# Layer 1's softmax sums taken from the product itself, its result turned by VectorE, and another order of tokens

## The chip, the cores and the metric

The kernel runs on one NeuronCore of a Trainium2 chip. The metric is the device time of one execution in microseconds (us), the median of several runs. Everything is float32. TensorE (PE) multiplies, VectorE (DVE) and ScalarE (ACT) do the elementwise work, GpSimd (POOL) does a few small operations, and SyncE (SP) issues every DMA of the program, one after the other in program order.

## The reference, cut to what is computed

Two layers over 4 images of 128 channels and 4096 places. Layer 0 is attention over the places with a gate and a projection; layer 1 is attention of the normalised tokens with themselves, and then a recurrent step over time.

```python
# layer 0
vg = sigmoid(conv_bn(gn(x), Wvg));  v, gate = split(vg)
q = conv_bn(gn(x), Wq) * SCALE;     k = conv_bn(gn(x), Wk)
attn = softmax(q^T k);              out = (v attn^T) * gate
x = x + conv_bn(out, Wp, sp, bp)
# layer 1
t = to_tokens(x)                                   # (4, 4096, 128)
h = layernorm(t);  q = h @ W;  t = t + softmax(q q^T) @ h
t = t + ffn(layernorm(t))                          # Wx, batch norm, y = sigmoid(wx_t + y V^T)
x = from_tokens(t)
```

Two facts are used below. Layer 1's scores are symmetric, so the exponentials of block (n, a) turned over are those of block (a, n). And a row of `h` is a layer norm without gain or bias, so its 128 channels sum to zero.

## The kernel before, in words

Each image b goes through `layer0` and then `layer1`; a recurrence over all images (from L814 on) ends the program. The 4096 places are 8 blocks of 512 (`QB`), each 4 tiles of 128.

`layer0` (L402 to L496) is a loop over query blocks n and 16 pairs of key tiles. Each pair is two score products into `ps` (L231), one exponential over 128x1024 (L233, ACT), a running sum of it (L240, DVE) and four products with the values into `o` (L426). After a block, `finish` (L433) appends six closures to the list `pending`, and later rounds of the loop take one each: `sums`, `denominators`, `projection`, `tokens`, and two called `nothing`, which give their place to the list `ahead` (preparation of the next image). `tokens` makes the tokens `t`, stores them to DRAM (L484) and writes their layer norm to `h`. Three times in a block, `move` (L263) turns a 128x512 tile over: DVE transposes 32x32 blocks into `d` (L269), one DMA writes `d` to a DRAM tile (L274), and four DMAs read it back in another order (L276). SP waits for the write before it issues the reads.

`layer1` (L498 to L740) goes over query blocks n in the order 6, 7, 5, 4, 3, 2, 1, 0 and over the key blocks a from n down to 0, with two rounds for each pair (n, a). A round has two score products (L695), two exponentials of 512 columns which also leave their row sums in `slots` (L701), and two products into `o` (L562) which lag two rounds behind. For a < n the exponentials are also turned over: DVE transposes them into `dd` (L706), 16 DMAs on SP carry `dd` to `tt` (L735), and four rounds later `reversed_products` makes four products with `tt` (L575), and DVE adds up all of `tt` for the other half of the softmax sums (L580). On the diagonal (a = n) the second round is `quarter` (L524), which computes a part of the scores and copies the rest from the round before.

`count` (L595) counts the parts of block n's output and its sums; when all are in, `finish` (L602) appends to `pending`: `tokens` (four transposes of the output L631, sum of `slots` L627, reciprocal, division and residual L633, layer norm), `result` (four transposes of the tokens by PE L644, an ACT copy L647, one DMA to `t2_d` L648), two `nothing`, `turn` (four transposes of the layer norm L653, an ACT copy L654) and `inputs` (one product L658, statistics L659, a copy L665 and its DMA L666). In the last image the blocks n < 4 have no `nothing`.

The program's text is not the order of an engine's instructions: a scheduler places them from priorities when the kernel is built, and each engine then runs its list in order.

Of the kernel before, what the change touches and what calls it, by code (L numbers as in the profile page):

```python
# [18 lines left out]
P = 128  # L19
# [30 lines left out]
def conv_attn_hybrid_kernel(  # L50
# [17 lines left out]
    turn_d = [dram.tile([P, 4, NQ, 32], F32, name=f"turn{i}_d") for i in range(8)]  # L68
# [60 lines left out]
    def scales():  # L129

        nc.vector.tensor_mul(w_v, w_v, bc[:, 0, :])
        nc.vector.tensor_mul(w_p, w_p, bc[:, 2, :])

        nc.vector.tensor_scalar(par2, par[:, SG : BG + 1], 0.5, None, ALU.mult)
# [31 lines left out]
def fast(  # L166
# [13 lines left out]
    with ExitStack() as st:  # L180
# [82 lines left out]
        def move(blocks, dst):  # L263

            nonlocal n_moves
            d = work.tile([P, 4, NQ, 32], F32, tag="d", name="d", bufs=2)
            turned = nc.vector.transpose(d.rearrange("q a j i -> q j a i"), blocks)  # L269
            if n_moves == 0:  # L270
                tc.keep_in_program_order(turned)
            via = turn_d[n_moves % len(turn_d)]
            n_moves += 1
            nc.sync.dma_start(via, d)  # L274
            for a in range(4):
                nc.sync.dma_start(dst[bass.ts(a, 32)], via[:, a].rearrange("(p i) j k -> i p j k", p=4))  # L276
# [18 lines left out]
        def tiles(t):  # L295

            return [t[:, :, j, :] for j in range(NQ)]

# [112 lines left out]
        def layer0(b, gate, q, k, v, need):  # L411
# [20 lines left out]
            def finish(n, o, acc):  # L432
# [12 lines left out]
                sub = stat.tile([P, NQ, 4], F32, tag="sub", name="sub", bufs=2)  # L445

                def sums():


                    half, blocks = acc[:, 0, :], acc[:, 1, :]  # L450
                    nc.vector.tensor_tensor(half, half, blocks, ALU.add)
                    nc.vector.transpose(blocks, half)
                    nc.vector.tensor_reduce(
                        sub, blocks.rearrange("q (j f k) -> q j f k", j=NQ, f=4), AX.X, ALU.add
                    )
                    move(xb.rearrange("c (j f k) -> c j f k", j=NQ, f=4), t)

                def denominators():
                    m0, m1 = halves(quart, sub.rearrange("q j f -> q (j f)"))
                    tot = stat.tile([P, NQ, 4], F32, tag="tot", name="tot", bufs=2)  # L460
                    flat = tot.rearrange("q j f -> q (j f)")
                    nc.vector.tensor_copy(flat, m0)
                    nc.vector.tensor_tensor(flat, flat, m1, ALU.add)
                    nc.vector.tensor_tensor(
                        tot, tot,
                        own.rearrange("q (j f) -> q j f", j=1).to_broadcast([P, NQ, 4]), ALU.mult,
                    )
                    den = den_all[:, b * NT + n * NQ : b * NT + (n + 1) * NQ]
                    nc.vector.tensor_reduce(den, tot, AX.X, ALU.add)
                    nc.vector.reciprocal(rinv, den)  # L470

                def projection():
# [3 lines left out]
                    move(og.rearrange("c (j f k) -> c j f k", j=NQ, f=4), yt)  # L476

                def tokens():
                    for j in range(NQ):
# [7 lines left out]
                    move(  # L487
                        h[:, ts, :].rearrange("q j (p i) -> q j p i", p=4),
                        qt[:, cs].rearrange("c (p j k) -> c p j k", j=NQ, p=4),
                    )  # L490
# [7 lines left out]
        def layer1(b, h, qt):  # L498
# [7 lines left out]

            slots = accp.tile([P, NT, NB + 1], F32, tag="slots", name="slots", bufs=2)
            nc.gpsimd.memset(slots[:, :, NB:], 0.0)
# [14 lines left out]
            def quarter(n, ps, e, before, slots):  # L523
# [14 lines left out]
                for half in range(2):  # L538
                    at = NQ * n + 2 + half
                    nc.scalar.activation(  # L540
                        e[:, half, hb:], ps[:, 0, bass.ts(half, hb)], AF.Exp, bias=shift,
                        accum_out=slots[:, at, n : n + 1],
                    )
                for half in range(2):
                    at = NQ * n + 2 + half
                    nc.scalar.activation(
                        e[:, half, :hb], ps[:, 1, bass.ts(half, hb)], AF.Identity,
                        accum_out=slots[:, at, NB : NB + 1],
                    )

            def order(n):


                return [1, 0] if b == B - 1 and n == 0 else list(range(n, -1, -1))
# [15 lines left out]
            def reversed_products():  # L570
# [3 lines left out]
                for j in range(NQ):  # L574
# [5 lines left out]
                nc.vector.tensor_reduce(  # L580
                    slots[:, bass.ts(n, NQ), a], t.rearrange("q p b k j -> q b p (k j)"),
                    AX.XY, ALU.add,
                )
                part(a, ot)
                count(n)

            def part(n, o):
# [5 lines left out]
                count(n)  # L593

            def count(n):  # L595


                parts[n] += 1
                if parts[n] == NB - (b == B - 1 and n == 0):
                    finish(n)  # L600

            def finish(n):  # L602
# [3 lines left out]
                if b == B - 1 and n == 0:  # L606
# [3 lines left out]
                    th, t2 = two[:, 0, :], two[:, 1, :]  # L610
# [3 lines left out]
                else:  # L614
# [3 lines left out]
                    t2 = None  # L618
# [5 lines left out]
                def tokens():  # L624
                    at = (B + b) * NT + n * NQ
                    den = den_all[:, at : at + NQ]
                    nc.vector.tensor_reduce(den, slots[:, bass.ts(n, NQ), :], AX.X, ALU.add)  # L627
                    nc.vector.reciprocal(rinv, den)
                    m = bank().rearrange("q (j c) -> q j c", j=NQ)
                    for j in range(NQ):  # L630
                        nc.tensor.transpose(m[:, j, :], oacc[:, n, bass.ts(j, P)], ident)  # L631
                    for j in range(NQ):
# [7 lines left out]
                def result():  # L640
                    nonlocal t2
                    m = bank()
                    for j in range(NQ):
                        nc.tensor.transpose(m[:, bass.ts(j, P)], t1[:, j, :], ident)  # L644
                    if t2 is None:
                        t2 = work.tile([P, QB], F32, tag="xb", name="t2")
                    nc.scalar.copy(t2, m)  # L647
                    nc.sync.dma_start(t2_d[b, :, cs], t2)  # L648

                def turn():  # L650
# [3 lines left out]
                    nc.scalar.copy(th, m)  # L654
# [13 lines left out]
                if b == B - 1 and n == 0:  # L668
                    pending.appendleft(tokens)
                    pending.extend([result, turn, inputs])  # L670
                elif b == B - 1 and n < 4:
                    pending.extend([tokens, result, turn, inputs])
                else:
                    pending.extend([tokens, result, nothing, nothing, turn, inputs])


            for n in [NB - 2, NB - 1] + list(range(NB - 3, -1, -1)):
# [4 lines left out]
                for a in order(n):  # L682
# [4 lines left out]
                    for i in range(2):  # L687
                        ps = ps_s.tile([P, 2, QB], F32, tag="s", name="ps")
                        e = ep.tile([P, 2, QB], F32, tag="e", name="e")
                        if a == n and i == 1:  # L690
                            quarter(n, ps, e, before, slots)
                        else:
                            for half in range(2):
# [4 lines left out]
                                )  # L698
                            for half in range(2):
                                at = NQ * a + 2 * i + half  # L700
                                nc.scalar.activation(  # L701
                                    e[:, half, :], ps[:, half, :], AF.Exp, bias=shift,
                                    accum_out=slots[:, at, n : n + 1],
                                )
# [19 lines left out]
                        if a > n and i == 1:  # L724
                            count(a)
# [571 lines left out]
```

## Time and profile before

| what | value |
|---|---|
| time, median of 3 runs | 3062.62 us (3060.75 to 3062.82) |
| the run that was profiled | 3064.04 us, span in the profile 3062.2 us |
| granted TensorE clock | 0.992 of full speed |
| ACT, busy | 1151.9 us (38%) |
| POOL, busy | 149.0 us (5%) |
| DMA moved | 241.16 MB, mean 79 GB/s |

Busy time of an engine is the union of its instructions. A group of the profile is all instructions of one line, engine, operation and tile, with its busy time, the mean of one instruction in ns, and the idle time of the engine just before them with what ended it. A float32 product of 128 by 512 stands in the trace as two records, so the 1160 records of L562 are 580 products.

### The profile page before, as it was taken

The numbers are of one execution on the slowest core, as the hardware profiler recorded it, in microseconds if no ns is written. First come the engines' busy times: TensorE is split into PE (matmuls) and PEld (weight loads), VectorE is DVE, ScalarE is ACT, GpSimd is POOL, SyncE is SP. The second block draws the span as 40 slices with busy tenths as digits, with TensorE's granted clock in tenths as the row PEclk, the third lists the DMA queues.
The fourth block names the chain that finished last, engine by engine and source line by source line (L and its number), as shares of the span: only waits on it lengthen the run. The fifth ranks groups of instructions, "written<-read, shape, count | busy, mean of one in ns | idle before, by whom it ended". The sixth has DMA issues, their size and how long they took to land.

```text
span 3062.2 us, 32664 instructions
## 1 busy us (share of the span) xinstructions
PE 3006.4 (98%) x10844; PEld 1382.7 (45%) x10844; DVE 1880.9 (61%) x3160; ACT 1151.9 (38%) x2147; POOL 149.0 (5%) x187
## 2 busy tenths in 40 slices
PE   8999999999999999999999999999999999999996
PEld 4444444444444444444444444444444444444443
DVE  6666665655666666555566666665566666455556
ACT  3443433333344443333344443333334444323334
POOL 0000000000000000000000000000000000000000
PEclk9999999999999999999999999999999999999998
DMA  1111143433111123333311113333321112543334
GB/s 42 38 56 56 49 112 87 99 89 97 48 56 56 47 80 94 92 97 91 82 47 61 42 49 110 89 96 95 93 59 57 41 50 93 138 102 93 100 104 166
DMA packets 233746, 241.16 MB, mean 79 GB/s; under 512 B 88544, under 2 KB 144352, under 8 KB 232544
## 3 DMA queue, kind: packets, MB, share of 16 engines
q1 hardware_dynamic: 233568, 238.97, 28.0%
q8 instruction: 89, 1.46, 0.2%
q14 instruction: 89, 0.73, 0.1%
HBM read 65.80 MB, written 56.62 MB: 40 GB/s over the span
## 4 chain that ended last, share of the span: by engine, by line
PE 95%; DVE 3%; issue 1%; ACT 1%; POOL 0%; DVEq 0%; POOLq 0%
PE o L426 29%; PE o L562 16%; PE ps L231 15%; PE ps L695 14%; PE ot L575 12%; PE m L260 1%; PE m L658 1%; PE mq L520 1%; PE ps L528 1%; PE mp L389 1%; PE mp L354 1%; PE mp L374 1%; DVE t2s L881 1%; DVE ps_r L854 1%; PE m L653 1%
## 5 line engine op out<-in xcount | busy, mean ns | idle before, releaser
L426 PE MATMUL o<-e,nxt 64*128 64x512 f32 x4096 | 966.2, 589 | 0.0
L233 ACT ACTIVATE e<-ps 128x1024 f32<-128x1024 f32 x512 | 520.8, 1023 | 685.2 <-PE ps L231 669.7
L240 DVE TENSOR_TENSOR acc<-acc,e 128x1024 f32<-128x1024 f32 x448 | 547.3, 1222 | 236.5 <-ACT e L233 220.8
L426 PEld LDWEIGHTS o<-e,nxt 64*128 64x128 f32 x4096 | 400.1, 187 | 483.0 <-issue 474.2
L701 ACT ACTIVATE e<-ps,shift 128x512 f32<-128x512 f32 x516 | 350.0, 683 | 675.0 <-PE ps L695 510.8
L562 PE MATMUL o<-e,h 128*128 128x512 f32 x1160 | 539.5, 592 | 0.0
L231 PE MATMUL ps<-nxt 64*128 64x512 f32 x2048 | 535.3, 596 | 1.2 <-DVE nxt L366 0.9
L695 PE MATMUL ps<-qt 128*128 128x512 f32 x1032 | 490.9, 595 | 2.9 <-ACT qt L521 2.7
L575 PE MATMUL ot<-tt,h 128*128 128x512 f32 x888 | 399.6, 593 | 0.2 <-DMA tt<-dd 0.2
L706 DVE STREAM_TRANSPOSE dd<-e 128x512 f32<-128x512 f32 x444 | 287.1, 687 | 85.9 <-ACT e L701 75.4
L562 PEld LDWEIGHTS o<-e,h 128*128 128x128 f32 x1160 | 218.2, 190 | 265.8 <-issue 261.2
L231 PEld LDWEIGHTS ps<-nxt 64*128 64x128 f32 x2048 | 194.2, 187 | 228.9 <-issue 151.3
L695 PEld LDWEIGHTS ps<-qt 128*128 128x128 f32 x1032 | 187.9, 190 | 213.5 <-issue 188.7
L575 PEld LDWEIGHTS ot<-tt,h 128*128 128x128 f32 x888 | 167.9, 190 | 210.4 <-issue 207.5
L580 DVE TENSOR_REDUCE slots<-tt 128x4 f32<-128x2048 f32 x111 | 250.8, 2259 | 9.3 <-DMA tt<-dd 8.9
L589 DVE TENSOR_TENSOR oacc<-oacc,ot 128x512 f32<-128x512 f32 x87 | 59.6, 685 | 188.3 <-PE ot L575 188.2
L138 POOL TENSOR_SCALAR rstd<-mv 128x4 f32<-128x4 f32 x64 | 14.5, 227 | 2349.7 <-DVE mv L287 2349.7
L701 ACT ACTIVATION_READ_ACCUMULATOR e<-ps,shift 128x1 f32 x516 | 101.3, 196 | 0.0
L443 POOL TENSOR_SCALAR xb<-xb,bpc 128x512 f32<-128x512 f32 x32 | 61.7, 1929 | 389.1 <-DMA xb<-in_x_dram 372.0
L480 DVE SCALAR_TENSOR_TENSOR t<-yt,rinv,t 128x128 f32<-128x128 f32 x128 | 36.5, 347 | 71.4 <-DMA yt<-turn_d 66.3
L139 POOL TENSOR_TENSOR rstd<-rstd,mhalf 128x4 f32<-128x4 f32 x64 | 66.4, 1037 | 5.3
L290 DVE TENSOR_SCALAR h<-t,mv,rstd 128x128 f32<-128x128 f32 x128 | 35.7, 342 | 47.1 <-POOL rstd L139 47.1
(161 smaller groups left out, 1667.3 us busy)
## 6 DMA issues: line engine op xcount, KB each, us to landing
tt<-dd SPq DMA_DIRECT2D x1776, 64.0 KB, 2.0
turn_d<-d SPq DMA_DIRECT2D x96, 256.0 KB, 2.0
t_d<-t SPq DMA_DIRECT2D x63, 256.0 KB, 2.0
xb<-in_x_dram SPq DMA_DIRECT2D x32, 256.0 KB, 2.9
t<-turn_d SPq DMA_DIRECT2D x128, 64.0 KB, 2.0
yt<-turn_d SPq DMA_DIRECT2D x128, 64.0 KB, 2.0
qt<-turn_d SPq DMA_DIRECT2D x128, 64.0 KB, 2.1
t<-t_d SPq DMA_DIRECT2D x32, 256.0 KB, 3.1
```

Of the source, the lines that this page charges most:

```text
L139: nc.gpsimd.tensor_tensor(dst, dst, mhalf[:, :n], ALU.pow)
L231: nc.tensor.matmul(ps[:, h, :], lhsT=lhsT, rhs=rhs, start=True, stop=True)
L233: nc.scalar.activation(e, ps, AF.Exp, scale=scale)
L240: nc.vector.tensor_tensor(acc, acc, e, ALU.add)
L426: nc.tensor.matmul(o[r], lhsT=v[rs, p + h * PAIRS, :], rhs=e[rs, h, :], start=(p == 0 and h == 0), stop=(p == PAIRS - 1 and h == 1),)
L443: nc.gpsimd.tensor_scalar(xb, xb, bpc, None, ALU.add)
L562: nc.tensor.matmul(o, lhsT=h[:, NQ * a + 2 * i + half, :], rhs=e[:, half, :], start=(a == order(n)[0] and i == 0 and half == 0), stop=(a = ...
L575: nc.tensor.matmul(ot, lhsT=h[:, NQ * n + j, :], rhs=t[:, :, j, :, :].rearrange("q p k j -> q k p j"), start=(j == 0), stop=(j == NQ - 1),)
L580: nc.vector.tensor_reduce(slots[:, bass.ts(n, NQ), a], t.rearrange("q p b k j -> q b p (k j)"), AX.XY, ALU.add,)
L695: nc.tensor.matmul(ps[:, half, :], lhsT=qt[:, bass.ts(at, P)], rhs=qt[:, bass.ts(n, QB)], start=True, stop=True,)
L701: nc.scalar.activation(e[:, half, :], ps[:, half, :], AF.Exp, bias=shift, accum_out=slots[:, at, n : n + 1],)
L706: nc.vector.transpose(d.rearrange("q f b k j -> q k b f j")[:, 2 * i + half], e[:, half, :].rearrange("q (b f j) -> q b f j", b=NQ, f=NQ),)
```

## The change

- `bpc`, the bias added to the residual of layer 0, has 1 subtracted once (DVE, one instruction), and after a block of `h` has been moved, POOL adds 1 to it in place (128x512). Every row of `h` then sums to 128, so the 128 channels of layer 1's output sum to 128 times the softmax sum: `tokens` of layer 1 takes the sum from there (a DVE reduction of the 128x512 output, a scaling, the reciprocal).
- `slots` and all that fills it are gone: the row sums of the exponentials, the DVE sum over `tt`, and the counting. An exponential is now one instruction of 128x1024, and `quarter` has two ACT instructions in place of four.
- A block of layer 1 is finished when its output is complete, without waiting for the sums.
- The tokens stand in another order in the 128 partitions, so that `move` is now: DVE transpose, four DMAs that write 512-byte runs to DRAM (`turn_out`), and one DMA that reads it back.
- `result` has no PE transposes and no ACT copy: DVE transposes the tokens into `d`, and four DMAs write them to `t2_d`. It is called at the end of `turn`, and a `nothing` takes its old place, so `turn` stays four places behind `tokens`. In the last image's blocks n < 4, `turn` moves from two places behind to one.
- `turn`'s ACT copy writes in another order. For the last block of the last image the key order is 0, 1 in place of 1, 0.

```diff
+        nc.vector.tensor_scalar(bpc, bpc, -1.0, None, ALU.add)
...
-            nc.sync.dma_start(via, d)
-            for a in range(4):
-                nc.sync.dma_start(dst[bass.ts(a, 32)], via[:, a].rearrange("(p i) j k -> i p j k", p=4))
+            for f in range(4):
+                nc.sync.dma_start(
+                    dst.rearrange("(a i) m -> i a m", a=4)[:, :, bass.ts(f, P)],
+                    d[bass.ts(f, 32)].rearrange("i a j k -> i a (j k)"),
+                )
+
+        def move(blocks, dst):
+            nonlocal n_moves
...
+            turn_out(blocks, via)
+            nc.sync.dma_start(dst, via)
...
+                    hn = h[:, ts, :].rearrange("q j c -> q (j c)")
+                    nc.gpsimd.tensor_scalar(hn, hn, 1.0, None, ALU.add)
...
-                for half in range(2):
-                    at = NQ * n + 2 + half
-                    nc.scalar.activation(
-                        e[:, half, hb:], ps[:, 0, bass.ts(half, hb)], AF.Exp, bias=shift,
-                        accum_out=slots[:, at, n : n + 1],
-                    )
...
+                nc.scalar.activation(
+                    e[:, :, hb:], ps[:, 0, :].rearrange("p (h q) -> p h q", h=2), AF.Exp,
+                    bias=shift,
+                )
+                nc.scalar.copy(e[:, :, :hb], ps[:, 1, :].rearrange("p (h q) -> p h q", h=2))
...
-                return [1, 0] if b == B - 1 and n == 0 else list(range(n, -1, -1))
+                return [0, 1] if b == B - 1 and n == 0 else list(range(n, -1, -1))
...
-                nc.vector.tensor_reduce(
-                    slots[:, bass.ts(n, NQ), a], t.rearrange("q p b k j -> q b p (k j)"),
-                    AX.XY, ALU.add,
-                )
                 part(a, ot)
-                count(n)
...
-                if parts[n] == NB - (b == B - 1 and n == 0):
+                if parts[n] == NB - n - (b == B - 1 and n == 0):
...
-                    nc.vector.tensor_reduce(den, slots[:, bass.ts(n, NQ), :], AX.X, ALU.add)
-                    nc.vector.reciprocal(rinv, den)
...
+                    nc.vector.tensor_reduce(den, m, AX.X, ALU.add)
+                    nc.vector.tensor_scalar(den, den, 1.0 / C, None, ALU.mult)
+                    nc.vector.reciprocal(rinv, den)
...
                 def result():
-                    m = bank()
-                    for j in range(NQ):
-                        nc.tensor.transpose(m[:, bass.ts(j, P)], t1[:, j, :], ident)
...
-                    nc.scalar.copy(t2, m)
-                    nc.sync.dma_start(t2_d[b, :, cs], t2)
+                    turn_out(t1.rearrange("q j (p i) -> q j p i", p=4), t2_d[b, :, cs])
...
-                    nc.scalar.copy(th, m)
+                    nc.scalar.copy(
+                        th.rearrange("c (p j k) -> c j p k", j=NQ, p=4),
+                        m.rearrange("c (j p k) -> c j p k", j=NQ, p=4),
+                    )
+                    result()
...
-                    pending.extend([tokens, result, turn, inputs])
+                    pending.extend([tokens, turn, inputs])
                 else:
-                    pending.extend([tokens, result, nothing, nothing, turn, inputs])
+                    pending.extend([tokens, nothing, nothing, nothing, turn, inputs])
...
-                                nc.scalar.activation(
-                                    e[:, half, :], ps[:, half, :], AF.Exp, bias=shift,
-                                    accum_out=slots[:, at, n : n + 1],
-                                )
+                            nc.scalar.activation(e, ps, AF.Exp, bias=shift)
```

## The prediction

> **What bounds the kernel now.** I read the page's busy times and slices, then its chain that ended last, then the groups, and last the instructions in order of time where the change cuts in. The first two say TensorE, throughout:
>
> ```profile
> PE 3006.4 (98%) x10844; PEld 1382.7 (45%) x10844; DVE 1880.9 (61%) x3160; ACT 1151.9 (38%) x2147; POOL 149.0 (5%) x187
> ...
> PE   8999999999999999999999999999999999999996
> ...
> PE 95%; DVE 3%; issue 1%; ACT 1%; POOL 0%; DVEq 0%; POOLq 0%
> ```
>
> Only the first and last slices are below nine tenths, and 95% of the chain is PE. So time that the change takes from DVE and ACT is worth something only where PE waits for them. The groups (with shapes kept apart) show how large that removed work is, and how little PE waits:
>
> ```profile
> L562 PE MATMUL o<-e,h 128*128 128x512 f32 x1160 | 539.5, 592 | 0.0
> L575 PE MATMUL ot<-tt,h 128*128 128x512 f32 x888 | 399.6, 593 | 0.2 <-DMA tt<-dd 0.2
> L580 DVE TENSOR_REDUCE slots<-tt 128x4 f32<-128x2048 f32 x111 | 250.8, 2259 | 9.3 <-DMA tt<-dd 8.9
> L695 PE MATMUL ps<-qt 128*128 128x512 f32 x1032 | 490.9, 595 | 2.9 <-ACT qt L521 2.7
> L701 ACT ACTIVATION_READ_ACCUMULATOR e<-ps,shift 128x1 f32 x516 | 101.3, 196 | 0.0
> L653 PE MATMUL m<-ident,h 128*128 128x128 f32 x124 | 21.1, 282 | 2.6 <-DVE h L290 2.2
> L644 PE MATMUL m<-ident,t1b 128*128 128x128 f32 x124 | 18.9, 275 | 0.0
> ```
>
> The last number of a line is PE's idle time ahead of the group: 0.0 for L562, 0.2 for L575, 2.9 for L695. The sum of all such waits in layer 1 is under 10 us. The line to look at is L644: PE work that the change removes. Its mean of 275 ns is no price, as overlapping instructions are counted each in full; the price is what the next product is put back by, read from PE in order of time:
>
> ```profile
> 2946.95 1.02 PE L695 MATMUL ps<-qt 128*128 128x512 f32 x2
> 2947.81 0.60 PE L644 MATMUL m<-ident,t1b 128*128 128x128 f32 x4
> 2948.25 1.88 PE L695 MATMUL ps<-qt 128*128 128x512 f32 x4
> ```
>
> Four transposes hold the stream from 2947.81 to 2948.25: 0.44 us. A product of 128x512 holds it 0.86 (2946.95 to 2947.81).
>
> **What the skill says.** The Trainium skill, Perfetto Trace Analysis, "Identifying the Most-Contended Engine", warns that matmul busy share does not measure the distance to a limit. Here starts of products follow at 0.43 us per record without gaps, so the stream is full and cutting instructions is what helps. The same page, "What 'DMA-bound' means", names the issuing sequencer as a limit of its own; SP in layer 1 is near that (below). DMA: Bandwidth & Descriptors, "Specifications", puts the smallest efficient transfer at 512 B; the new writes are just that long, and the old reads of 512 B landed in 2.0 us. SBUF — State Buffer, "Who interferes with whom", says that DVE and GpSimd share one pair of ports as an exclusive lock; no line of this trace shows a DVE instruction held up by it.
>
> **The change part by part.** Counts of added and removed instructions are those of the built kernel's lists.
>
> 1. *PE transposes of `result`.* 32 groups of four go: 128 instructions fewer, and nothing else changes in PE's counts. 31 groups lie in the full stream: 31 x 0.44 = 13.6 us off. The last lies in the tail (part 6).
>
> 2. *ACT and DVE relief in layer 1.* DVE loses 111 x 2.259 = 251 us, ACT 516 x 0.196 = 101 us of accumulator reads plus 516 x 0.683 - 258 x 1.023 = 88 us by the merge (1.023 from L233, the same shape). DVE gains 32 transposes (0.71, as L269) and 32 reductions of 128x512 (0.69, as L453): 45 us. All of it lies beside PE. In the stream PE stalls before a turn (L653) for 0.8 us twice and 1.1 once in the last image, and 1.0 once per image before L354; some may go. Bounds 0 to 5 us gained; I take 0, since the next point takes a like amount.
>
> 3. *The turn nearer to its product.* In the built kernel's PE order, the turn's transposes mostly come 8 to 29 us of PE work after those of `tokens`, so the layer norm is ready (two exceptions in the tail). But `inputs` (was L658) now follows the turn mostly after one product, 0.86 us; it was mostly three or more. The trace has such a case: last transpose of L653 at 2952.49, product of L658 at 2953.46, 0.97 us with ACT free at once, and PE filled this exactly with a transpose and a product. If ACT has an exponential (1.02) running, PE waits for its rest. ACT is busy under a third of the time. Per block 0 to 1.0 us, so 0 to 32 us at the very worst; I take 0.05 x 31 = 1.5.
>
> 4. *`move` and the POOL addition in layer 0.* `move` keeps five DMAs. Before: write 0.34 to issue, 2.0 to land, four issues of 0.43, 2.0 to land: 6.1 us. After: 4 x 0.43 + 2.0 + 0.34 + 2.0 to 3.1 (3.1 is `t<-t_d`, the same 256 KB): 6.1 to 7.2. DVE already waits for `yt` 66.3 us in 31 waits, and PE's idle time at L426 is 0.0: four buffers of `e` hide this wait, and half a microsecond more. POOL's addition to `h` is 32 x 1.93 (L443, same shape): it follows the move's transpose and is read first in layer 1, many rounds later; were DVE locked out for all 62 us, layer 0 has DVE a third idle. Queued behind it on POOL are only the residual of a next block and the layer norms' two small operations. Value 0, bounds 0 to 10 us lost.
>
> 5. *SP's queue in layer 1.* `result` had one issue of 0.33, now four of about 0.43: 1.4 us more per block, in front of the `tt<-dd` issues. SP's order in time shows why this matters:
>
> ```profile
> 568.01 10.02 SPq L735 DMA_DIRECT2D tt<-dd  x16
> 582.26 0.33 SPq L648 DMA_DIRECT2D t_d<-t  x1
> 582.69 21.78 SPq L735 DMA_DIRECT2D tt<-dd  x32
> ```
>
> Sixteen issues take 10 us, and PE's two rounds with their reversed products take 12 x 0.86 = 10.3. From the landing of the sixteenth DMA to the first product that reads `tt`, I measure for each of the 111 turned blocks 3 to 14 us in all but one (0.2 at 2670.9 us; there PE waits 0.4). A block's diagonal gives SP about 5 us back, more than 1.4. And SP no longer stands behind an ACT copy for `result` (142.6 us of waiting for L647), since the new transpose is done long before. Value 0, bounds 0 to 4.
>
> 6. *The tail.* From the end of the last product of L562 (2961.3) to block 0's normalising on DVE:
>
> ```profile
> 2962.81 0.68 DVE L589 TENSOR_TENSOR oacc<-oacc,o 128x512 f32<-128x512 f32 x1
> 2964.25 1.13 DVE L633 SCALAR_TENSOR_TENSOR last<-ml,rinv,t 128x128 f32<-128x128 f32 x4 [0.75 <-PE ml L631]
> 2969.74 1.11 DVE L290 TENSOR_SCALAR last<-last,mv,rstd 128x128 f32<-128x128 f32 x4 [0.90 <-POOL rstd L139]
> ```
>
> That is 8.4 us. In the built kernel block 1's steps end there too. Its transposes come 4.3 us (five products) before the end. Then DVE: latency 0.3, reduction, scaling and reciprocal 0.9, L633 1.1, statistics 1.2, transpose into `d` 0.7: 4.2, so block 0's sum L589 starts at once, not 1.5 late. But block 1's normalising waits for POOL (1.5) and ends at 6.9 on this clock. Then block 0: 0.9 + 1.1 + 1.2 + 0.7 + POOL 1.5, and block 1's `inputs` 1.4 in between, 0.2 for the check of the sums: 13.9, less 4.3 = 9.6. So 1.2 us lost. After that the chain is as before. Bounds: 1 gained, 3 lost. At the start, the one instruction on `bpc` stands beside a DMA that DVE waits for already: 0.1 at most.
>
> Sum against the profile's own span: 3062.2 - 13.6 + 1.5 + 1.2 = 3051.3, 10.9 us less. The profiled run lies within 0.05% of the three runs (3060.75 to 3062.82), so from their median: 3062.6 - 10.9 = **3051.7**.
>
> **The rivals.**
> - *More comes off than PE's instructions* (DVE's and ACT's relief removes most stalls of points 2 and 6, none arise): 3062.6 - 13.6 - 6 = 3043. For it: 251 us of long DVE instructions go. Against: PE's idle column.
> - *The gain is eaten by waits of `inputs` for ACT*: with a wait of 0.35 us in each of 31 blocks, 3062.6 - 13.6 + 11 + 1.2 = 3061. For it: the distance of 0.86 is below the measured 0.97, and one exponential now takes 1.02 at a stretch where it was 0.68. Against: ACT is mostly idle.
> - *SP's queue becomes the bound of layer 1* and the time ends above before. The place is the `tt<-dd` issues behind the four writes; the price 1.4 us for each of 31 blocks, 43 us in all, and it decides once the 3 to 14 us between landing and use are spent, that is if what each diagonal gives back is less than what the block adds. If two thirds is lost: 3062.6 - 13.6 + 1.2 + 29 = 3079. Against: the slack recovers within each block in the trace of before.
>
> **How the numbers follow.** Chances: the forecast (3046 to 3057) 0.68, more off (below 3046, around 3043) 0.12, eaten (3057 to 3069) 0.12, SP or another queue (above) 0.08. The range leaves out the SP case and the far ends of the others: 3042 to 3062. What this measurement can tell from no change is 0.2%, 6.1 us: faster means below 3056.5. That is the forecast and the larger gain, 0.80; within 0.2% 0.12; slower 0.08.
>
> **What would show it.** In the changed profile: PE's busy time about 13 us lower with its share still at 98%; no L644; DVE's near 1,675 us (1881 - 251 + 45); the idle column of the new `inputs` and `ot<-tt` products below 2 us each; the span from the last `o<-e,h` product to block 0's normalising near 9.6 us. I am wrong if PE idles before `ot<-tt` on DMA, or before `m<-th` on ACT, by 5 us or more.

## The result and the profile after

| | before | after |
|---|---|---|
| time, median (lowest to highest) | 3062.72 us (3060.75 to 3065.87) | 3051.56 us (3051.15 to 3052.10) |
| ratio, 95% interval | | 0.9963 (0.9945 to 0.9980) |
| span of the profiled run | 3062.2 us | 3049.4 us |

The forecast was 3051.7 us. The page after, its busy times, the slices of PE and the chain that ended last:

```profile
PE 2991.0 (98%) x10716; PEld 1370.4 (45%) x10716; DVE 1676.6 (55%) x3114; ACT 1032.5 (34%) x1149; POOL 218.4 (7%) x215
...
PE   8999999999999999999999999999999999999985
...
PE 93%; DVE 3%; SPq 2%; ACT 1%; DMA 1%; issue 0%; POOL 0%; DVEq 0%; ACTq 0%
```

PE is still the bound: 128 instructions and 15.4 us fewer, the share still 98%. DVE lost 204 us and ACT 119 us, and PE's slices don't show it. The 2% of SPq in the last line is no loss of that size: the chain runs back through SP's queue from 1203 us on, from the one wait of PE that is put down to `tt<-dd`, and that wait lasted 0.8 us. The groups of PE after, kept apart by shape (name, count | busy us, mean ns | idle time before them):

```profile
L564 PE MATMUL o<-e,h 128*128 128x512 f32 x1160 | 537.0, 592 | 0.0
L685 PE MATMUL ps<-qt 128*128 128x512 f32 x1032 | 482.9, 594 | 2.7 <-ACT qt L530 2.7
L577 PE MATMUL ot<-tt,h 128*128 128x512 f32 x888 | 400.9, 593 | 0.0
L648 PE MATMUL m<-th,w 128*128 128x512 f32 x62 | 34.9, 645 | 0.7 <-ACT th L640 0.7
L639 PE MATMUL m<-ident,h 128*128 128x128 f32 x124 | 22.0, 282 | 1.9 <-DVE h L298 1.9
L622 DVE TENSOR_REDUCE den_all<-m 128x4 f32<-128x512 f32 x31 | 21.4, 689 | 14.9 <-PE m L619 14.9
```

No group of the removed L644 is left. The reversed products (L577, was L575) don't wait for their DMAs at all, and `inputs` (L648, was L658) waits 0.7 us for ACT in the whole program, once, behind the last product of L564. The last line is the new sum from the output, 0.69 us each as the prediction took it. SP in layer 1, in order of time (start, us, issues):

```profile
565.51 10.25 SPq L719 DMA_DIRECT2D tt<-dd  x16
575.86 2.01 SPq L274 DMA_DIRECT2D t_d<-d  x4
582.50 0.59 SPq L656 DMA_DIRECT2D wxs_d<-wx  x1
583.19 41.79 SPq L719 DMA_DIRECT2D tt<-dd  x64
```

The four writes take 2.0 us here, 0.50 each and not the 0.43 of the estimate, and a pause follows before the next issue: the queue has room for them.

**Where the time went.** I divide the span by PE's order of time: the start until the first product with the values in layer 0 (L437), a *stream* from there to the end of the last L564, then the way to block 0's normalising, from there to the first product of the recurrence (L851), and the rest. The stream is divided once more. Its *own work* is the number of records times the interval at which such records follow each other without a gap (0.429 us for 128x512, 0.2145 for 64x512 and 128x256, 0.109 for a transposition of 128x128). What remains is waits, and switches between products of 128 rows and of 64. Own work is thus a count times an interval; only the sum of the two lines is measured.

| us | before | after | difference |
|---|---|---|---|
| start | 29.6 | 27.8 | -1.8 |
| stream, own work | 2879.6 | 2866.5 | -13.1 |
| stream, waits and switches | 52.1 | 50.7 | -1.4 |
| last product to normalising | 8.45 | 10.14 | +1.7 |
| normalising to recurrence | 10.0 | 10.9 | +0.9 |
| recurrence and end | 82.4 | 83.4 | +1.0 |

They sum to -12.7, the difference of the two spans. The start isn't the change's: in a second profile of the same changed kernel it was 29.1, with a stream equal to 0.1 us.

### The profile page after: what moved, and what is told of

It is laid out like the page before. It is cut to its first block, busy times and chain, and to the rows that moved or that the text cites. A ratio compares the mean times of both kernels' runs of the same rounds, so it can differ in the third digit from the quotient of the medians.

```text
span 3049.4 us, 31514 instructions
## 1 busy us (share of the span) xinstructions
PE 2991.0 (98%) x10716; PEld 1370.4 (45%) x10716; DVE 1676.6 (55%) x3114; ACT 1032.5 (34%) x1149; POOL 218.4 (7%) x215
## 4 chain that ended last, share of the span: by engine, by line
PE 93%; DVE 3%; SPq 2%; ACT 1%; DMA 1%; issue 0%; POOL 0%; DVEq 0%; ACTq 0%
PE o L437 28%; PE o L564 15%; PE ps L233 14%; PE ps L685 14%; PE ot L577 12%; SPq L719 2%; PE m L262 1%; PE m L648 1%; PE mp L400 1%; PE ps L537 1%; PE mp L365 1%; PE mq L529 1%; PE mp L385 1%; DVE t2s L865 1%; DVE ps_r L838 1%; PE m L639 1%
## 5 line engine op out<-in xcount | busy, mean ns | idle before, releaser
L437 PE MATMUL o<-e,nxt 64*128 64x512 f32 x4096 | 972.9, 589 | 0.0
L437 PEld LDWEIGHTS o<-e,nxt 64*128 64x128 f32 x4096 | 403.3, 187 | 483.0 <-issue 474.2
L233 PE MATMUL ps<-nxt 64*128 64x512 f32 x2048 | 542.4, 595 | 2.0 <-DVE nxt L377 0.9
L564 PE MATMUL o<-e,h 128*128 128x512 f32 x1160 | 537.0, 592 | 0.0
L689 ACT ACTIVATE e<-ps,shift 128x1024 f32<-128x1024 f32 x258 | 287.4, 1114 | 646.6 <-PE ps L685 357.1
L685 PE MATMUL ps<-qt 128*128 128x512 f32 x1032 | 482.9, 594 | 2.7 <-ACT qt L530 2.7
L577 PE MATMUL ot<-tt,h 128*128 128x512 f32 x888 | 400.9, 593 | 0.0
L564 PEld LDWEIGHTS o<-e,h 128*128 128x128 f32 x1160 | 218.8, 190 | 268.3 <-issue 268.0
L577 PEld LDWEIGHTS ot<-tt,h 128*128 128x128 f32 x888 | 167.8, 190 | 210.2 <-issue 205.1
L140 POOL TENSOR_SCALAR rstd<-mv 128x4 f32<-128x4 f32 x64 | 14.6, 228 | 2380.0 <-DVE mv L295 2380.0
L491 DVE SCALAR_TENSOR_TENSOR t<-yt,rinv,t 128x128 f32<-128x128 f32 x128 | 36.4, 346 | 77.4 <-DMA yt<-turn_d 77.4
L502 POOL TENSOR_SCALAR h<-h 128x512 f32<-128x512 f32 x32 | 72.4, 2261 | 63.8 <-DVE d L270 61.7
L547 ACT ACTIVATE e<-ps,shift 128x512 f32<-128x512 f32 x32 | 22.0, 687 | 143.8 <-PE ps L543 126.3
L588 DVE COPY oacc<-ot 128x512 f32<-128x512 f32 x24 | 16.6, 692 | 85.1 <-PE ot L577 85.0
```

The source lines that it names most:

```text
L233: nc.tensor.matmul(ps[:, h, :], lhsT=lhsT, rhs=rhs, start=True, stop=True)
L437: nc.tensor.matmul(o[r], lhsT=v[rs, p + h * PAIRS, :], rhs=e[rs, h, :], start=(p == 0 and h == 0), stop=(p == PAIRS - 1 and h == 1),)
L502: nc.gpsimd.tensor_scalar(hn, hn, 1.0, None, ALU.add)
L564: nc.tensor.matmul(o, lhsT=h[:, NQ * a + 2 * i + half, :], rhs=e[:, half, :], start=(a == order(n)[0] and i == 0 and half == 0), stop=(a = ...
L577: nc.tensor.matmul(ot, lhsT=h[:, NQ * n + j, :], rhs=t[:, :, j, :, :].rearrange("q p k j -> q k p j"), start=(j == 0), stop=(j == NQ - 1),)
L685: nc.tensor.matmul(ps[:, half, :], lhsT=qt[:, bass.ts(at, P)], rhs=qt[:, bass.ts(n, QB)], start=True, stop=True,)
```

## The experiments

Times are medians; the ratio is to the kernel before in runs beside them, where it took 3064.1, 3064.3 and 3063.6 us in three sets. The changed kernel measured again beside them took 3051.84 us, ratio 0.9959 (0.9945 to 0.9973).

> The changed kernel once more, as the yardstick for the three runs beside it. 3051.6 us measured so far; 3049 to 3054 expected, and a span within 3 us of it. The start of layer 0's first product is expected anywhere from 27.8 to 30.4 us, as the profiles so far spread.

The other columns are of each kernel's own profile: the stream, its waits and switches, and two parts of these. *Beside steps* is what lies directly before or after layer 1's `tokens`, `result`, `turn` and `inputs` in PE's order, worked out from start to start: how much later the next group begins than the records before it take by their intervals. *Idle* is PE's idle time in the stream before the transposes of the layer norm in `turn` (`m<-ident,h`), with the number of waits. The last column is the way from the last L564 to the first product of the recurrence, the *tail*.

| kernel | us | ratio (95%) | stream | waits and switches | beside steps | idle `m<-ident,h` | tail |
|---|---|---|---|---|---|---|---|
| before | 3062.7 | | 2931.7 | 52.1 | 14.5 | 2.2 (3) | 18.5 |
| after | 3051.6 | 0.9963 (0.9945-0.9980) | 2917.2 | 50.7 | 14.8 | 1.6 (3) | 21.0 |
| dead_pe | 3081.4 | 1.0058 (1.0041-1.0074) | 2945.0 | 65.4 | 28.1 | 2.7 (3) | 22.4 |
| pe_result | 3067.4 | 1.0012 (1.0005-1.0018) | 2935.2 | 53.9 | 20.6 | 0.6 (1) | 17.4 |
| slots_back | 3076.9 | 1.0043 (1.0026-1.0060) | 2938.6 | 72.5 | 33.8 | 4.0 (10) | 22.9 |
| order_only | 3064.1 | 0.9999 (0.9990-1.0008) | 2932.6 | 53.0 | 14.6 | 2.2 (3) | 17.5 |
| sp16 | 3058.1 | 0.9981 (0.9974-0.9988) | 2924.0 | 57.5 | 17.7 | 3.3 (4) | 21.2 |
| tail_pe | 3051.8 | 0.9959 (0.9944-0.9973) | 2917.7 | 50.7 | 14.9 | 1.6 (3) | 21.0 |
| halves | 3050.0 | 0.9954 (0.9938-0.9971) | 2916.5 | 50.0 | 14.1 | 1.5 (3) | 19.4 |
| halves_all | 3052.6 | 0.9962 (0.9949-0.9976) | 2917.9 | 51.4 | 14.1 | 1.5 (3) | 20.2 |
| dve_load | 3064.0 | 0.9999 (0.9991-1.0008) | 2926.0 | 59.5 | 23.7 | 2.8 (6) | 23.3 |
| count_late | 3062.2 | 0.9995 (0.9986-1.0003) | 2926.4 | 59.9 | 20.4 | 6.6 (7) | 20.8 |
| slots_place | 3058.9 | 0.9985 (0.9978-0.9992) | 2923.9 | 57.4 | 16.7 | 1.6 (6) | 21.5 |

**The theory at first:** the gain is PE's removed transposes, 0.44 us for each group, and the relief of DVE and ACT is worth nothing. Its rival: the relief is where the gain comes from. Three kernels were to tell them apart.

*dead_pe* is after, with the removed transposes done as well; nothing reads their result.

```diff
                 def result():
+                    m = bank()
+                    for j in range(NQ):
+                        nc.tensor.transpose(m[:, bass.ts(j, P)], t1[:, j, :], ident)
                     turn_out(t1.rearrange("q j (p i) -> q j p i", p=4), t2_d[b, :, cs])
```

> The changed kernel, with the four PE transposes of the tokens added back in front of result's DVE transpose, into a PSUM bank that nothing reads; all else stays, so the output is unchanged. Theory 'PE instructions' (the time is the length of TensorE's stream): 31 groups in the stream x 0.44 to 0.47 us, about 14 us more than the changed kernel's 3051.6: 3064 to 3067. Rival 'relief' (the gain is the DVE and ACT work that went, PE's transposes were hidden): 3051 to 3054.

*pe_result* is after, with `result` by PE, ACT and one DMA in its old place between `tokens` and `turn`.

```diff
-                    turn_out(t1.rearrange("q j (p i) -> q j p i", p=4), t2_d[b, :, cs])
+                    m = bank()
+                    for j in range(NQ):
+                        nc.tensor.transpose(m[:, bass.ts(j, P)], t1[:, j, :], ident)
+                    t2 = ...
+                    nc.scalar.copy(...)
+                    nc.sync.dma_start(t2_d[b, :, cs], t2)
...
-                    result()
...
-                    pending.extend([tokens, nothing, nothing, nothing, turn, inputs])
+                    pending.extend([tokens, result, nothing, nothing, turn, inputs])
```

> The changed kernel with one part undone: result again by four PE transposes, an ACT copy (in the new order of tokens) and one DMA, in its old place one behind tokens; the softmax sums still come from the product. Theory 'PE instructions': 14 us more in the stream, about 1 us less in the tail: 3062 to 3066. Rival 'relief': 3050 to 3054. Rival 'SP queue' (the four DMAs of result cost time): below the theory, by up to 1.4 us for each of 31 blocks where they bind.

*slots_back* is after, with the softmax sums by ACT's accumulators and DVE's sum of `tt` as before, no one added to `h`, the old condition for a finished block and the old key order of the last one.

```diff
-                            nc.scalar.activation(e, ps, AF.Exp, bias=shift)
+                            for half in range(2):
+                                nc.scalar.activation(
+                                    e[:, half, :], ps[:, half, :], AF.Exp, bias=shift,
+                                    accum_out=slots[:, at, n : n + 1],
+                                )
...
+                nc.vector.tensor_reduce(
+                    slots[:, bass.ts(n, NQ), a], t.rearrange("q p b k j -> q b p (k j)"),
+                    AX.XY, ALU.add,
+                )
                 part(a, ot)
+                count(n)
```

> The changed kernel with the other part undone: row sums by ACT in slots and the DVE sum over tt are back, one is not added to the values, blocks finish when the sums are in and the last key order is 1, 0 again; result stays on DVE. Theory 'PE instructions': the 251 us of DVE and 190 us of ACT come back beside PE and only the last image's stalls (some 5 us) return, while the tail is 1 to 2 us shorter without the reductions: 3051 to 3057. Rival 'relief': the whole gain is gone, 3060 to 3064.

All three came out above both theories' numbers: 29.8 us over after for the dead transposes (12 to 15 expected), 15.8 for `result` by PE (10.5 to 14), and 25.3 for the sums (up to 5, or 8 to 12). Either part of the change undone puts the kernel above where both are undone. So neither price alone is the answer. For the first of them, PE of dead_pe in order of time at the border of layer 1 and the next image's layer 0:

```profile
776.52 1.02 PE L564 MATMUL o<-e,h 128*128 128x512 f32 x2
777.38 0.63 PE L636 MATMUL m<-ident,t1b 128*128 128x128 f32 x4
777.95 1.12 PE L233 MATMUL ps<-nxt 64*128 64x512 f32 x2
779.00 1.12 PE L651 MATMUL m<-th,w 128*128 128x512 f32 x2
...
783.06 1.02 PE L233 MATMUL ps<-nxt 64*128 64x512 f32 x4
783.92 1.88 PE L437 MATMUL o<-e,nxt 64*128 64x512 f32 x8
...
789.26 1.01 PE L642 MATMUL m<-ident,h 128*128 128x128 f32 x4 [0.89 <-DVE h L298]
790.20 1.12 PE L233 MATMUL ps<-nxt 64*128 64x512 f32 x2
791.25 0.66 PE L636 MATMUL m<-ident,t1b 128*128 128x128 f32 x4
791.84 0.69 PE L233 MATMUL ps<-nxt 64*128 64x512 f32 x1
```

Here the group holds PE from 777.38 to 777.95 and from 791.25 to 791.84, 0.57 and 0.59 us and not 0.44. And twice two records of score products of 64 rows stand alone, from 777.95 to 779.00 and from 790.20 to 791.25: 1.05 us for two, where four in a row take 0.86 (783.06 to 783.92). So at this border a group costs more than the 0.44 read in layer 1, and it can cost 0.6 us more at its neighbours (1.05 less half of 0.86). Own work accounts for 13.1 of dead_pe's loss in the stream, the other 14.7 are waits and switches, and 13.3 of these lie beside steps.

**Are the parts independent?** *order_only* undoes both parts, the edits of slots_back and of pe_result together, and keeps the new order of tokens and the new moves.

> Both main parts undone, the new order of tokens and the new moves of layer 0 kept: sums from slots with two exponentials of 512 columns, result by PE and ACT in its old place. Theory A (the parts are independent, so the losses seen when each part alone is undone add up): 15.8 us for the result and 25.3 us for the sums on top of 3051.6, so about 3093 us. Theory B (the turn by VectorE is only dear while VectorE also carries the 251 us of sums; the order of tokens itself costs nothing): close to before, 3060 to 3068 us. A value of 3070 to 3085 would say that the order of tokens or the new moves cost something by themselves.

3064.06 us, as before (ratio 0.9999): the order of tokens and the moves together cost nothing, and the losses don't add. The four kernels with the new order of tokens make a square:

| us | `result` by PE, old place | `result` by DVE, end of `turn` |
|---|---|---|
| with `slots` | 3064.1 | 3076.9 |
| sums from the output | 3067.4 | 3051.6 |

Turning by DVE costs 12.8 us beside the slots and saves 15.8 without them. The new sums alone give nothing, 3.3 us lost. Both differences hold a stream and a tail: the stream becomes 6.0 us longer beside the slots and 18.0 shorter without them, while the tail becomes longer both times, by 5.3 and 3.7. The second theory, that follows from it: the turn by DVE needs DVE's relief. Waits of PE in slots_back and in order_only (engine, tile and line <- what it waited for: us in the whole program, times, longest):

```profile
PE m L651 <- DVE h L297: 7.9, 11, 3.9
...
PE m L632 <- DVE wx L667: 4.1, 3, 1.4
```

```profile
PE m L659 <- DVE h L297: 2.2, 3, 0.9
```

With `result` by PE the slots leave PE 2.2 us of waits for the layer norm. With `result` by DVE it is 7.9 in 11 waits, and 4.1 more where a transposition of `tokens` waits for DVE to copy the `inputs` of the block before out of their bank. The longest of the 11 lies in the tail:

```profile
2973.68 1.11 PE L651 MATMUL m<-ident,h 128*128 128x128 f32 x4 [3.95 <-DVE h L297]
```

So these waits are 5.9 of the 19.5 us by which the stream's waits and switches differ (72.5 to 53.0). That is little because idle time shows only a part: a record of 128x512 stands in the trace for 0.59 us where the next can begin after 0.43, and a wait inside that is not seen. From start to start, 19.2 of the 19.5 us lie beside steps (33.8 to 14.6), 9.4 of them at the transposes of the layer norm.

**Which part of the slots does it?** Three kernels took them apart. *dve_load* is after with only DVE's sums back, into a tile that nothing reads.

```diff
+                nc.vector.tensor_reduce(
+                    sums[:, bass.ts(n, NQ), a], t.rearrange("q p b k j -> q b p (k j)"),
+                    AX.XY, ALU.add,
+                )
                 part(a, ot)
```

> As after, with VectorE's sum over each turned tile back (111 times 128x2048, 251 us in all) into a tile that nothing reads; ScalarE stays merged and no block waits for a sum. Theory 'load': VectorE's work beside the stream is what makes the turn by VectorE dear, because the layer norms reach PE late: most of the 25 us that the slots cost beside the turn by VectorE come back, 3066 to 3077 us, and PE idles before the layer norm's transposes by 5 us or more. Theory 'schedule': it is when a block is finished and where the steps are placed: 3050 to 3057.

*count_late* is after with only the old condition for a finished block.

```diff
                 part(a, ot)
+                count(n)
...
-                if parts[n] == NB - n - (b == B - 1 and n == 0):
+                if parts[n] == NB - (b == B - 1 and n < 2):
```

> As after, but a block is taken as finished only when its turned tiles have been used as well, as before the change (the tokens step then comes some 9 to 14 us later); no sums are made. Theory 'schedule': the later finish pushes the steps of the last blocks into the next image's layer 0, where full-row transposes cost more: 3060 to 3077 us, with 3 to 6 us more per image. Theory 'load': 3050 to 3056.

*slots_place* is slots_back with `result`, still by DVE, as a step of its own in the old place.

```diff
-                    result()
...
-                    pending.extend([tokens, nothing, nothing, nothing, turn, inputs])
+                    pending.extend([tokens, result, nothing, nothing, turn, inputs])
```

> As slots_back (3076.9 us), but the result's turn by VectorE is a step of its own in the old place between tokens and turn instead of standing at the end of turn. Theory 'place': VectorE's transposition in the turn is what delays the next instructions there, and the old place gives back at least half of the loss: 3050 to 3065. Theory 'load' or 'schedule': the place doesn't matter, 3070 to 3080.

DVE's load alone costs 12.4 us (8.9 in the stream, 2.2 in the tail), the later finish alone 10.6 (9.2 in the stream). Together that is 23.0 of the 25.3 of slots_back, but that the two add isn't shown, and what ACT's accumulators cost wasn't tried alone. Neither of the theories "load" and "schedule" has all of it: count_late came out where "schedule" expected it, and dve_load between the two, 2 us below what "load" expected, with less idle time before the layer norm than the 5 us that "load" asked for. The waits for the layer norm in dve_load, in count_late and in slots_place:

```profile
PE m L644 <- DVE h L298: 3.6, 7, 0.8
```

```profile
PE m L642 <- DVE h L298: 7.0, 8, 1.1
...
PE m L622 <- DVE wx L658: 1.6, 3, 0.5
```

```profile
PE m L651 <- DVE h L297: 2.9, 7, 1.3
```

The last wait of each, 0.8, 0.4 and 1.3 us, lies in the tail. In dve_load the reversed products wait for no DMA, so the sum that holds `tt` longer doesn't hold up the turned tiles; and from start to start 8.6 of the stream's 8.9 us lie at the transposes of the layer norm, which is the place that "load" named.

In count_late DVE has no more to do than in after, and PE waits 6.6 us for `h` in the stream where it waited 1.6. What is different is when the steps come. In the first image, PE's transposes of `tokens` begin at 618.8, 675.1, 714.3 and 743.4 us in after and at 628.3, 680.5, 719.6 and 753.0 in count_late (which started 2.2 later): three to seven us later beyond that, as a block waits for its last turned tile. So block 1's turn (at 775.7 us) falls among the first score products of the next image's layer 0, where in after (768.0) it lies in layer 1, and its transposes, of all 128 rows, break those up. That is 2.4 of the 6.6 us; another 3.2 come at the turn before it (747.5 us), which lies in layer 1 and isn't explained by this.

slots_place shows that the place matters as much: with all of the slots, the old place of `result` gives back 18 us of the 25.3, and beside steps 16.7 us are left of 33.8. The theory "place" holds, with one reservation: the same edit takes away one of three `nothing`, that is a turn of the next image's preparation, which wasn't tried alone. So what costs 25 us is not the slots as such but the slots with DVE's transposition at the end of `turn`. After with `result` in the old place wasn't run, so whether the new place is good without the slots stays open. In slots_place against order_only, only `result` by DVE differs, and 5.1 us are saved of 13.1 of own work: the stream is 8.7 us shorter, the tail 3.9 longer.

**ACT.** *halves* is after with two exponentials of 512 columns per round, as before but without sums; *halves_all* also splits the diagonal.

```diff
-                            nc.scalar.activation(e, ps, AF.Exp, bias=shift)
+                            for half in range(2):
+                                nc.scalar.activation(e[:, half, :], ps[:, half, :], AF.Exp, bias=shift)
```

> As after, but each exponential of layer 1 off the diagonal is again two instructions of 512 columns, without the row sums; the diagonal's stays merged. It separates ScalarE's relief from VectorE's. Theory 'VectorE's 251 us made room, ScalarE's relief is worth nothing': 3050 to 3054 us, PE stalls as in after. Theory 'fewer ScalarE instructions took part in it': 3055 to 3062 us with PE waiting for ScalarE ahead of the products of e or of the next block. A gain is possible too, as half a block of exponentials is ready 0.3 us sooner and a small copy on ScalarE waits for 0.68 us at most in place of 1.02: 3047 to 3050.

> As halves (3050.0 us), with the diagonal's exponential and copy on ScalarE in two parts as well, without sums. If PE's wait for ScalarE's copy at the start of the next image's layer 0 (0.3 us in three images in after) goes, 3048 to 3050; if the merge on the diagonal is worth nothing either way, 3049.5 to 3051.5. Either would be no more than 0.15% from after.

3049.97 and 3052.57 us, on either side of after. halves_all is 1.1 us above the higher of its two expectations, halves at the border of two of its own. The merge is worth nothing either way; halves is the lowest median here, but 1.9 us are within the spread of after's own runs (3050.58 to 3053.47), and I don't call it faster. The profiles agree: the stream is 2916.5 in halves, 2917.9 in halves_all and 2917.2 in after.

**SP.** *sp16* writes `result` with sixteen DMAs of a quarter's size in place of four (`step` is 1 there, and 4 in `move`).

```diff
             for f in range(4):
-                nc.sync.dma_start(... dst[:, :, bass.ts(f, P)], d[bass.ts(f, 32)])
+                for a in range(0, 4, step):
+                    nc.sync.dma_start(... dst[:, a : a + step, bass.ts(f, P)], d[bass.ts(f, 32), a : a + step])
```

> The changed kernel with result's four DMAs cut into sixteen of 128 runs in all (same bytes and same 512-byte runs), so that SP issues 12 more for each block, about 12 x 0.3 to 0.43 = 4 to 5 us. Theory 'SP has slack' (3 to 14 us between landing and use, the diagonal gives 5 back): within 3 us of the changed kernel, 3050 to 3055. Rival 'SP is at its bound': 4 to 5 us for each of 24 to 31 blocks, 3120 and more.

3058.07 us: 6.5 over after, between the two expectations. The reversed products of sp16:

```profile
L579 PE MATMUL ot<-tt,h 128*128 128x512 f32 x888 | 401.1, 593 | 2.2 <-DMA tt<-dd 1.9 <-issue 0.3
```

Twelve more issues per block bring one wait of PE for `tt`, 1.9 us, in the whole program: SP is not at its bound, but its slack isn't free either. DVE waits 77.2 us for DMAs before it may overwrite `dd` (34.2 in after). Of the 6.9 us by which the stream is longer 2.9 lie beside steps; I didn't follow the rest.

**The tail.** *tail_pe* is after, with the last image's blocks 1 and 0 turned by PE in the old place.

```diff
                 def result():
+                    if not (b == B - 1 and n < 2):
+                        turn_out(...)
+                        return
+                    ...   # transposes, copy, one DMA, as before
```

> As after, but in the last image blocks 1 and 0 of layer 1 have their result turned by PE, copied by ACT and stored by one DMA, in the old place of that step. Theory 'the tail was mis-sized': the way from the last direct product to the recurrence's first product (21.05 us in after, 18.48 before) comes back to 18 to 19.5, for 0.44 us of PE work in the stream: 3048 to 3050.5 us. Theory 'the tail is set by the layer norm of blocks 1 and 0 and not by the extra transposition on VectorE': 20.5 to 22 us and a time of 3051 to 3054.

3051.78 us, as after: the first theory falls. The way from the last product to the recurrence is 21.0 us, as in after. So DVE's transposition in these two blocks isn't what makes the tail longer. The tail of after, in order of time (the last L564 ends at 2944.92):

```profile
2945.12 0.69 DVE L586 TENSOR_TENSOR oacc<-oacc,o 128x512 f32<-128x512 f32 x1 [0.37 <-PE o L564]
2946.22 1.11 DVE L298 TENSOR_SCALAR h<-t1b,mv,rstd 128x128 f32<-128x128 f32 x4 [0.42 <-POOL rstd L141]
2947.26 0.68 DVE L622 TENSOR_REDUCE den_all<-ml 128x4 f32<-128x512 f32 x1
...
2948.45 0.86 DVE L626 SCALAR_TENSOR_TENSOR last<-ml,rinv,t 128x128 f32<-128x128 f32 x3
...
2950.39 0.70 DVE L649 BATCH_NORM_STATS2 bn_st<-m 128x6 f32<-128x512 f32 x1 [1.08 <-PE m L648]
2951.01 0.67 DVE L652 COPY wxs<-m 128x512 f32<-128x512 f32 x1
2951.60 0.34 DVE L626 SCALAR_TENSOR_TENSOR last<-ml,rinv,t 128x128 f32<-128x128 f32 x1
...
2955.06 1.11 DVE L298 TENSOR_SCALAR last<-last,mv,rstd 128x128 f32<-128x128 f32 x4 [0.58 <-POOL rstd L141]
2955.46 1.24 PE L639 MATMUL ml<-ident,last 128*128 128x128 f32 x4 [5.11 <-DVE last L298]
```

Block 1's layer norm (2946.22) and its `inputs` (L649, L652) stand in DVE's list inside block 0's chain, and the fourth division of block 0 waits behind them from 2949.3 to 2951.60. In tail_pe they stand before the new sum L622 instead, and cost the same. With `result` by PE in all blocks the tail is 17.4 us (pe_result), and there block 1's layer norm is done before the last L564 ends (2964.07):

```profile
2958.30 1.12 DVE L298 TENSOR_SCALAR h<-t1b,mv,rstd 128x128 f32<-128x128 f32 x4 [1.47 <-POOL rstd L141]
2964.27 0.69 DVE L586 TENSOR_TENSOR oacc<-oacc,o 128x512 f32<-128x512 f32 x1 [1.29 <-PE o L564]
```

So the tail may be set by where block 1's steps fall rather than by what they contain; that wasn't tried alone.

## Why the prediction came out right, step by step

1. *PE's transposes*, 13.6 us off. The stream's own work fell by 13.1, as 30 of the 31 groups stood in the stream of before; block 1's of the last image came behind its last product. The price of 0.44 was read at one place in layer 1; six of the 30 stood among products of 64 rows, where a group takes 0.59 (from 791.47 to 792.06 us in before). And the kernels show that this is not what the part brings in every kernel: beside the slots it is 5.1 in the old place and 12.8 lost at the end of `turn`.

2. *ACT's and DVE's relief*, value 0 and bounds 0 to 5 gained. This is the step whose reason was wrong. Measured against before it seemed right, for the sums alone (pe_result) give no gain. But I costed it beside a kernel in which PE turns the result. With DVE turning at the end of `turn`, dve_load loses 12.4 us: there the relief is the condition of the first step. The bounds should have been drawn for the parts together. It also gave no price to a block's being finished earlier, which is worth 10.6 us in count_late, nearly as much as 251 us of DVE's work. ACT's part was rightly nothing (halves), though its size was wrong: 101 + 88 us were to go, and ACT lost 119 in all. In before, the accumulator reads overlap the exponentials, so that without them L701 and L540 would be busy for 27 us less, not 101 and more; and a merged exponential takes 1.11 us, not 1.02.

3. *The turn nearer to its product*, 1.5 us lost. L648 waits for ACT only in the tail (0.7 us). All waits and switches of the stream together fell by 1.4. Two kinds of wait rose, at the start of the next image's layer 0, here PE after in order of time:

```profile
762.51 1.12 PE L233 MATMUL ps<-nxt 64*128 64x512 f32 x2 [0.26 <-ACT e L551]
...
781.83 1.10 PE L639 MATMUL m<-ident,h 128*128 128x128 f32 x4 [0.54 <-DVE h L298]
```

   Both come once after each of the first three images, 0.26 and 0.54 us, so 2.4 us of the 3.5 by which waits and switches behind products of 64 rows rose. All others of the stream fell, by 4.9, and steps 2 and 3 together, +1.5 by the prediction, were -1.4.

4. *`move` and POOL*, value 0: order_only, which has the new moves and no addition on POOL, is as fast as before. The addition takes 2.26 us and not 1.93; DVE waits 77.4 us for `yt` instead of 66.3, and PE's idle time before the products of `e` (L437) is still 0.0.

5. *SP's queue*, value 0: L577 waits for nothing. Twelve more issues per block would cost 6.5 us (sp16).

6. *The tail*, 1.2 us lost, 9.6 from the last product to block 0's normalising: 10.1, so 1.7 lost. The 0.9 that follow are twelve transposes of the recurrence, in before, in after and in halves, where PE's work is the same as in after:

```profile
2975.60 4.33 PE L831 MATMUL ps_r<-wxs,ident 128*128 128x256 f32 x12 [1.47 <-DVE wxs L662]
```

```profile
2960.92 5.21 PE L815 MATMUL ps_r<-wxs,ident 128*128 128x256 f32 x12 [1.47 <-DVE wxs L652]
```

```profile
2960.66 4.38 PE L817 MATMUL ps_r<-wxs,ident 128*128 128x256 f32 x12 [1.47 <-DVE wxs L652]
```

   So the change's work on PE doesn't explain it, though both profiles of the changed kernel have it; it stays open. The end after the recurrence took 26.5 to 28.5 us in these profiles, 27.5 and 28.5 in two of the changed kernel; I don't explain its 1.0.

Of the rivals, "more comes off" would have needed the waits to fall by 6 us, "eaten" 11 us of waits of `inputs` (0.7 measured), and "SP" waits before `ot<-tt` (0.0). The forecast of 10.9 us stands against 11.2 between the medians. Part of that closeness is luck: 0.5 us less in own work, a gain of 2.9 more in the stream's waits, 1.4 more lost in the tail to the recurrence, and a start and an end that differ from profile to profile by 2 us and more each.

## What to carry to other kernels

In this kernel, whose PE has almost no gaps, removed PE instructions came off one for one only where what takes over their work had room at the very place where it is put. So price the parts of a change together, in the kernel in which all are made; undoing one part doesn't measure that part. A line that says when a block counts as finished weighed 10.6 us here, and where one step stands in a list 18, as against 12.4 for 251 us of work beside the stream.

## What the runs showed of the hardware

- A group of four transposes of 128 rows takes 0.44 us among products of 128 rows and 0.57 to 0.59 beside products of 64 rows, and two records of 64-row score products left alone take 1.05 us where four in a row take 0.86.
- PE's stream is reproducible to 0.1 us in two profiles of the same kernel (2917.2 and 2917.1), so small differences are better read there than in the time, in which the start alone moves by 2.6 us (27.8 to 30.4).
- PE's idle time in the trace shows only a part of its waits: in dve_load the stream is 8.9 us longer than in after, and its listed waits for the layer norm there are 1.2 us longer.
- The same twelve transposes of the recurrence, after PE has idled, took 4.3 to 5.4 us from profile to profile.
